# A two-layer graph network with experts on one core: empty rows written between row fetches, and four steps of the routing put elsewhere

## The chip, the cores and the metric

The kernel runs on one core of a Trainium2 chip. The metric is the device time of one execution in microseconds (us); given are the median of the runs and their lowest and highest. A profile of one further execution shows what each engine did. TensorE (PE) does the matmuls, PEld is its loading of weights, VectorE (DVE) and ScalarE (ACT) do elementwise work, GpSimd (POOL) does small work and issues the indirect DMAs, SyncE (SP) issues the plain DMAs.

## The reference

There are N = 2708 nodes with D = 256 features, an adjacency matrix, and E = 8 experts. Each of two layers adds an attention and a mixture of experts to x, each on a normalised x:

```python
    x = x + _L0_gnn_ref(_layernorm(x), adj, ...)    # softmax(q k' / 16 where adj > 0) @ v, then elu
    x = x + _L0_ffn_ref(_layernorm(x)[None], ...)   # 2 of 8 experts, hidden 1024, own layernorm
    x = x + _L1_gnn_ref(_layernorm(x), adj, ...)    # softmax(s_i + s_j + b where adj > 0) @ H
    x = x + _L1_ffn_ref(_layernorm(x)[None], ...)   # 2 of 8 experts, hidden 512
```

An expert is `gelu(x @ W1 + b1) @ W2 + b2`. A gate (x @ Wr, or x @ gate_w) ranks the experts for each node; the two best are applied and their results are added with softmax weights (layer 0: over the two; layer 1: over all eight).

## The kernel before

**Tiles and stages.** The nodes lie in NT = 22 tiles of 128 rows (P), the last with 20. The program runs through layer 0's attention (`layer0_attention`, L293), layer 0's experts, layer 1's attention (`layer1_attention`, L587) and layer 1's experts; two objects of the class `Experts`, `experts0` and `experts1`, hold the experts' parts. `own_norm` is true for layer 0's experts and false for layer 1's.

**Layer 1's attention.** Groups of 6, 6, 4, 3 and 3 tiles of queries are accumulated in PSUM at a time. For each tile of keys k, `attend` issues three matmuls for every query tile of the group (L660: mask times three parts of the values). At a group's end `evict` copies the sums out and gives the group's tiles to the routing (`finish`, which leads into `route`).

**Routing in steps.** `route` (L834) is a generator; each `yield` ends a step. An object of the class `Line` (L264) holds the waiting and the running generators, and each `line.step()` advances every running one by one step and starts a new one at set gaps. In the attention a `line.step()` stands behind the matmuls of each k; in the experts' slots two stand in each slot. So routing and matmuls are woven together by the order of the program. The steps of one tile of nodes are: statistics (L200 to L206; the power L206 is on POOL); the rows written, with the token numbers by POOL (L854) and a copy of the first row into the second (L858, DVE); the gate's logits, the two best and their numbers (L878 to L884) and the exp of the weights (L885, ACT); an empty step; the counting of places by two small matmuls (L899 with `sel`, L900 with `seen`), which share one PSUM tile; and then L901 to L914 on DVE, `seen` being updated by L908, and two indirect scatters by POOL (L917) of the rows into the DRAM buffer `disp`. In `disp` each expert has a region of CAP rows, filled from its start. The row tiles have 4 buffers (pool `routing`), so L854 and L858 of a tile wait for the scatters of an earlier one.

**Tables.** An expert's rows are worked off in slots of 128 rows. `place(s0, s1)` (L924) computes from the counts `seen` (one matmul, L930, then DVE) for the slots s0 to s1 which expert (`weight_row`) and which rows of `disp` (`token_row`) they take. It runs twice for each layer. The early call comes from `begin()` (L1028) in the attention, as soon as 16 tiles (layer 0) or 14 tiles (layer 1) have been routed, for the first n = 24 or 20 slots; these hold only full chunks of rows. `begin` also fetches the rows and weights of slots 0 to 2. The late call comes in a slot, when the routing is finished or when slot n is about to be fetched, for the slots from n on. As an expert's last chunk may be partly filled, the late call also writes, behind the last row of each of the eight experts, 128 rows of "nobody" (L937 to L943: for each expert a register load of the end on SP, L938, and a DMA of 129 KB on SP, L943).

**Slots.** There are up to 50 slots (SLOTS). The weights of a slot lie in one of 4 ring buffers, its rows `xg` in one of 6. Slot s does: `up` (L1128: matmuls `mm`, 16 in layer 1; L1121: the bias copied on ACT; L1136: gelu into `hT` on ACT); a routing step; perhaps `place`; in layer 1 `turned(s + 1)`, which transposes the next slot's rows (L1105, `tp`) and copies them out (L1115 on ACT, `xe`); `down` of slot s - 1 (L1144, eight matmuls in layer 1), with `fetch()` inside; `y` (L1150, L1151 on DVE) and a scatter on POOL (L1155 in layer 1); a routing step. `fetch()` fetches for slot s + 3 (AHEAD) the weights (L1057, indirect, POOL) and the rows (L1067 a register load and L1072 the DMA, SP). The fetch of slot n waits until everything that was written to `disp` has landed; the slots from 3 to n - 1 don't, because their rows are known to be complete. Exp and gelu use different tables of ACT, so an exp between two gelus brings an ACT_TABLE_LOAD ahead of the exp and another ahead of the next gelu.

**What sets the order.** Every engine works off its instructions in order. SP's order is that of the program text everywhere (L74), and in layer 1's slots so are those of PE, ACT and DVE (L1088). Everywhere else a planner of the framework orders each engine's instructions by costs and dependencies.

Of the kernel before, what the change touches and what calls it, by code (L numbers as in the profile page):

```python
# [14 lines left out]
AF = mybir.ActivationFunctionType  # L15
# [4 lines left out]
P = 128  # L20
N = 2708
D = 256
DC = D // P
E = 8
# [24 lines left out]
CAP = (NT + 1) * P  # L49
# [4 lines left out]
AHEAD = 3  # L54
# [6 lines left out]
def adj_ffn_kernel(ctx: ExitStack, tc: tile.TileContext, a: dict, out: bass.AP):  # L61
    nc = tc.nc
# [53 lines left out]
    nobody = const.tile([P, DROW], F32, name="nobody")  # L116
# [470 lines left out]
    def layer1_attention(mTs, kept, line):  # L587
        with ExitStack() as scope:
# [102 lines left out]

            ahead = [normed_rows(t) for t in range(2)]
            cols = columns(0, ahead.pop(0))
            g0, total = 0, None
            for g, wide in enumerate(GROUPS):
                if g == 1:


                    n = FULL_AFTER[experts1.early]
                    experts1.open([i * (n // RING) * E // (n + GROUP) for i in range(RING)])  # L700
                ts_ = list(range(g0, g0 + wide))
                accs = [ps_acc.tile([P, VALUES + 1], F32, name="acc") for _ in ts_]

                line.gap = NT // wide
                for k in range(NT + (LAG1 if g == 0 else 0)):
                    if g == 0:
                        if k + 2 < NT:
                            ahead.append(normed_rows(k + 2))
                        if k < NT:
                            now = cols  # L710
                            if k + 1 < NT:
                                cols = columns(k + 1, ahead.pop(0))
                            values(k, now)
                        if k >= LAG1:
                            attend(ts_, k - LAG1, accs)
                    else:
                        attend(ts_, k, accs)
                        line.step()
                    if g > 0:
                        if not experts1.begun and experts1.routed >= experts1.early:  # L720
                            experts1.begin()
                if g == 0:
                    sums = pool.tile([P, DC], F32, name="sums", bufs=1)
                    nc.vector.tensor_reduce(sums, sums_of, AX.X, ALU.add)
                    total = all_sum(pool, sums, wfc, VALUES, "total1")
                    nc.vector.tensor_add(
                        logits, logits, bfc_gate.unsqueeze(1).to_broadcast([P, NT, E])
                    )
                evict(ts_, accs, total)
                g0 += wide  # L730
# [39 lines left out]
    class Experts:  # L770
        def __init__(self, layer, hidden, packed_weights, w_gate, gate_bias, own_norm, xd, disp, early):
            self.hidden, self.packed_weights, self.own_norm = hidden, packed_weights, own_norm
            self.w_gate, self.gate_bias, self.xd, self.disp = w_gate, gate_bias, xd, disp

            self.seen = const.tile([P, E], BF16, name=f"seen{layer}")
            nc.vector.memset(self.seen, 0.0)
            self.routed, self.begun = 0, False
            self.written = []
            self.groups = [f"written{layer}", f"late{layer}", f"apart{layer}", f"after{layer}"]
            self.early = early  # L780


            n = FULL_AFTER[early]

            size = -(-(SURE - n) // RING)
            runs = [(0, 0, n // RING, 1), (n, size - 1, size, -1)]
            self.number = const.tile([P, SLOTS, 2], F32, name=f"number{layer}")
            number_i = const.tile([P, SLOTS], I32, name=f"number_i{layer}")
            for s0, c0, size, step in runs:
                nc.gpsimd.iota(  # L790
                    number_i[:, s0 : s0 + size * RING], pattern=[[step, size], [size, RING]],
                    base=c0, channel_multiplier=0,
                )
            s0 = n + size * RING
            nc.gpsimd.iota(
                number_i[:, s0:], pattern=[[1, SLOTS - s0]], base=s0 - n, channel_multiplier=0
            )
            nc.vector.tensor_copy(self.number[:, :, 0], number_i)
            nc.vector.tensor_scalar(
                self.number[:, :, 1], self.number[:, :, 0], float(P), None, ALU.mult  # L800
            )
# [32 lines left out]
        def route(self, t, x, logits=None):  # L834


            own_norm, xd, disp, seen = self.own_norm, self.xd, self.disp, self.seen
            w_gate, gate_bias = self.w_gate, self.gate_bias
            r = ROWS[t]
            rows2 = [routing.tile([P, DROW], F32, name=f"row{j}") for j in range(2)]  # L840
# [12 lines left out]
            for j in range(2):  # L853
# [1 line left out]
                    rows2[j].bitcast(I32)[:r, D : D + 1],  # L855
                    token[:r, 0 if own_norm else j, t : t + 1],
                )
            nc.vector.tensor_copy(rows2[1][:r, :D], rows2[0][:r, :D])  # L858
            yield
            lg = small.tile([P, E], F32, name="lg")  # L860
            if logits is None:
# [19 lines left out]
            k = 2 if own_norm else E  # L881
            p = small.tile([P, E], F32, name="p")
            den = small.tile([P, 2], F32, name="den")
            nc.vector.tensor_scalar(p[:r], best[:r], best[:r, 0:1], None, ALU.subtract)  # L884
            nc.scalar.activation(p[:r, :k], p[:r, :k], AF.Exp, accum_out=den[:r, 0:1])  # L885

            hot = small.tile([P, 2, E], F32, name="hot")
            nc.vector.tensor_tensor(
# [5 lines left out]
                nc.vector.memset(sel, 0.0)  # L894
            nc.vector.tensor_add(sel[:r], hot[:r, 0], hot[:r, 1])
            yield
            yield
            ps = misc.tile([P, GROUP, P], F32, name="misc").rearrange("p g n -> p (g n)")
            nc.tensor.matmul(ps[:, :E], before, sel, start=True, stop=False)  # L899
# [21 lines left out]
                )  # L921
            self.routed += 1

        def place(self, s0, s1):  # L924


# [6 lines left out]
            if all_chunks:  # L933

                end = one.tile([P, E], I32, name="end")
                nc.vector.tensor_add(end, n_e, regions)
                for e in range(E):  # L937
                    at = nc.values_load(  # L938
                        end[0:1, e : e + 1], min_val=e * CAP, max_val=e * CAP + N,
                        engines=(mybir.EngineType.SP,),  # L940
                        skip_runtime_bounds_check_because="an expert has at most N tokens",
                    )
                    self.other_rows(nc.sync.dma_start(disp[bass.ds(at, P), :], nobody))  # L943
            tab = one.tile([P, NT, E], F32, name="tab")
            nc.vector.tensor_tensor(
                tab, n_e.unsqueeze(1).to_broadcast([P, NT, E]),
# [20 lines left out]
            n = s1 - s0  # L967
# [129 lines left out]
        def slots(self, two, ps_mm, ps_tp, ps_acc, line):  # L1097
# [20 lines left out]
            def up(w, xe):  # L1118

                bias2 = two.tile([P, D], F32, name="bias2")  # L1120
                (nc.vector.tensor_copy if own_norm else nc.scalar.copy)(bias2, w[:, b2:b1])  # L1121
                hT = two.tile([P, hc, P], F32, name="hT")
                for g in range(0, hc, GROUP):
                    ps = ps_mm.tile([P, GROUP, P], F32, name="mm")
                    for i in range(GROUP):
                        f = g + i
                        for c in range(DC):
                            nc.tensor.matmul(  # L1128
                                ps[:, i, :],
                                w[:, c * hidden + f * P : c * hidden + (f + 1) * P],  # L1130
                                xe[:, c, :],
                                start=(c == 0), stop=(c == DC - 1),
                            )
                    for i in range(GROUP):
                        f = g + i
                        nc.scalar.activation(  # L1136
                            hT[:, f, :], ps[:, i, :], AF.Gelu, bias=w[:, b1 + f : b1 + f + 1]
                        )
                return hT, bias2
# [34 lines left out]
            def slot(s, s1):  # L1174
                nonlocal placed, behind, xe
                w, xg = self.fetched[s]
                if own_norm:
                    xe = turned(s)
                hT, bias2 = up(w, xe)
                line.step()  # L1180

                def fetch():
                    if s + AHEAD < SLOTS and s + AHEAD == len(self.fetched):
                        self.fetched.append((self.fetch_weights(s + AHEAD), self.fetch_rows(s + AHEAD)))

                if not placed and (not line.busy() or s + AHEAD == n):

                    line.finish()
                    self.place(n, SLOTS)
                    placed = True  # L1190

                if s + 1 < s1 and not own_norm:
                    xe = turned(s + 1)
                if behind is None:
                    fetch()
                else:
                    down(*behind, fetch)
                line.step()
                behind = (s, w, xg, hT, bias2)
                if s % 5 == 4 and background:  # L1200
                    background.pop(0)()
# [114 lines left out]
```

## Time and profile before

| | |
|---|---|
| time, median of 3 runs | 1356.41 us (1351.57 to 1359.59) |
| profiled execution, its own time | 1355.36 us |
| span of that execution | 1353.7 us |
| TensorE's mean granted clock | 0.965 |
| busy: PE, DVE, POOL, ACT | 1245.3, 552.6, 415.3, 379.8 us |

The stages lie in that span roughly so: layer 0's attention to 590 us, layer 0's experts to 872, layer 1's attention to 1111, layer 1's experts with routing beside them to 1158, the late tables and the slots around them to 1183, the other slots to 1298, and the end, with the sum of the two parts of each node and the output, to 1353.7.

How to read it: busy times say how much an engine did, not that it was waited for. In the table by windows each row is a stretch of the span, with the time that each engine was busy in it, its granted clock, and the share in which the DMA engines moved data. In the views of groups and of the timeline the square bracket or the last column gives the idle time of the engine just before, and what ended it. The chain of waits goes back from the last instruction through what released each step.

### The profile page before, as it was taken

Reading aid. Unit: us, or ns where it says so; the run is one execution under the profiler, and the core shown is the slowest. Engines: PE = TensorE matmul, PEld = TensorE weight load, DVE = VectorE, ACT = ScalarE, POOL = GpSimd, SP = SyncE. Lnnn points to the kernel's source line nnn. Section 1 sums busy time; section 2 is a strip of 40 time slices with the busy share of each in tenths; the row PEclk is TensorE's granted clock in tenths of the full one; section 3 lists DMA queues with packets and bytes.
Section 4 is the critical chain, followed back from the end, with each engine's and each line's share of the span. In section 5 each row is a group of like instructions: output and inputs, shape, how many; then the busy total and the mean of one; then the engine's idle time right before and its main releaser. Section 6 shows DMA issues by size and latency. Waiting matters only on the chain. (4 is left out here: it accounts for less than half of the span.)

```text
span 1353.7 us, 21527 instructions
## 1 busy us (share of the span) xinstructions
PE 1245.3 (92%) x7536; PEld 973.9 (72%) x7536; DVE 552.6 (41%) x2145; ACT 379.8 (28%) x1134; POOL 415.3 (31%) x523
## 2 busy tenths in 40 slices
PE   7999999999999999999999999879999887599990
PEld 4676666666566666899999999756887647599880
DVE  5723743635527344521221222176546527322124
ACT  3222222212212222633233233234200016344440
POOL 5200110111111212533333333342143437355550
PEclk8899999999999998999999999979999999899995
DMA  6700354997938427275669454360010115434557
GB/s 214 252 5 27 131 178 120 260 230 211 229 89 200 100 68 312 54 240 151 207 210 342 115 165 110 97 223 1 1 40 25 36 52 180 147 102 125 171 173 253
DMA packets 106059, 197.86 MB, mean 146 GB/s; under 512 B 26017, under 2 KB 80374, under 8 KB 99802
## 3 DMA queue, kind: packets, MB, share of 16 engines
q1 hardware_dynamic: 75740, 109.41, 28.4%
q0 software_dynamic: 27392, 84.24, 19.7%
q10 hardware_dynamic: 2814, 2.77, 0.6%
q8 instruction: 62, 1.02, 0.3%
q14 instruction: 51, 0.42, 0.1%
HBM read 263.63 MB, written 66.12 MB: 244 GB/s over the span
## 5 line engine op out<-in xcount | busy, mean ns | idle before, releaser
L1128 PE MATMUL mm<-xe,ring 128*128 128x128 f32 x2192 | 273.8, 279 | 16.9 <-ACT xe L1115 11.6
L1128 PEld LDWEIGHTS mm<-xe,ring 128*128 128x128 f32 x2192 | 264.5, 194 | 33.4 <-ACT xe L1115 14.8
L1144 PE MATMUL acc<-ring,hT 128*128 128x256 f32 x1096 | 267.6, 382 | 3.5 <-ACT hT L1136 3.5
L1136 ACT ACTIVATE hT<-mm,ring 128x128 f32<-128x128 f32 x548 | 156.6, 369 | 256.0 <-issue 185.8
L1144 PEld LDWEIGHTS acc<-ring,hT 128*128 128x128 f32 x1096 | 195.8, 191 | 23.9 <-ACT hT L1136 4.2
L432 PE MATMUL s<-g,xnT 128*128 128x512 f32 x420 | 206.8, 607 | 6.2 <-DVE mT L444 6.2
L489 PE MATMUL acc<-v,p 128*128 128x257 f32 (+1 forms) x880 | 209.0, 389 | 0.0
L1150 DVE TENSOR_TENSOR y<-acc,bias 128x256 f32<-128x256 f32 x92 | 39.0, 424 | 370.3 <-PE acc L1144 357.8
L660 PE MATMUL acc<-parts,mT 128*128 128x265 bf16 (+1 forms) x1386 | 174.5, 282 | 2.1 <-POOL parts L635 1.3
L660 PEld LDWEIGHTS <-mT 128*128 128x128 fp8e4 (+1 forms) x1386 | 132.6, 99 | 49.9 <-issue 22.4
L489 PEld LDWEIGHTS acc<-v,p 128*128 128x128 f32 (+1 forms) x880 | 153.1, 190 | 18.1 <-issue 0.8
L1057 POOL DMA_INDIRECT ring<-L_ffn_packed,weight_row x98 | 104.1, 1062 | 191.7 <-issue 153.2
L206 POOL TENSOR_TENSOR ln_rs<-ln_rs,minus_half 128x2 f32<-128x2 f32 x88 | 67.8, 776 | 237.6 <-DVE ln_rs L202 201.0
L917 POOL DMA_INDIRECT disp<-row,to x88 | 88.1, 1001 | 145.8 <-issue 58.4
L444 DVE TENSOR_SCALAR mT<-s 128x512 fp8e4<-128x512 f32 x105 | 72.0, 687 | 135.1 <-ACT p L443 135.0
L432 PEld LDWEIGHTS s<-g,xnT 128*128 128x128 f32 x420 | 75.8, 193 | 52.8 <-issue 42.1
L443 ACT ACTIVATE p<-s 128x512 f32<-128x512 f32 x105 | 62.2, 595 | 166.6 <-PE s L438 166.4
L1162 POOL DMA_INDIRECT xd<-y,xg x45 | 71.0, 1577 | 87.1 <-PE mm L1128 27.7
L438 PEld LDWEIGHTS <-apart 128*128 128x128 fp8e4 x420 | 32.5, 98 | 60.9 <-issue 60.9
L327 DVE TENSOR_SCALAR apart<-adj 128x677 fp8e4<-128x677 int32 x80 | 40.6, 512 | 50.5 <-DMA adj<-in_adj_dram 43.6
L1155 POOL DMA_INDIRECT xd<-y,xg x47 | 47.2, 1005 | 18.4 <-PE tp L1105 7.0
L854 POOL COPY row<-token 128x1 int32<-128x1 int32 (+1 forms) x88 | 17.4, 209 | 104.2 <-DMA disp<-row,to 103.3
(230 smaller groups left out, 1135.5 us busy)
## 6 DMA issues: line engine op xcount, KB each, us to landing
adj<-in_adj_dram SPq DMA_DIRECT2D x84, 338.5 KB
L_ffn_packed<-in_L_ffn_W_dram SPq DMA_DIRECT2D x16, 1024.0 KB
xg<-disp SPq DMA_DIRECT2D x98, 129.0 KB
L_ffn_packed<-in_L_ffn_W_dram SPq DMA_DIRECT2D x16, 512.0 KB
neighbours<-mT SPq DMA_DIRECT2D x5, 1408.0 KB
mT<-neighbours SPq DMA_DIRECT2D x5, 1408.0 KB
xin<-in_x_dram SPq DMA_DIRECT2D x42, 128.0 KB
ring<-L_ffn_packed SPq DMA_DIRECT2D x4, 1154.0 KB
```

The source lines that it names most:

```text
L206: nc.gpsimd.tensor_tensor(rs[:r, 1], rs[:r, 0], minus_half[:r], ALU.pow)
L432: nc.tensor.matmul(ps[:kr, :nb], xnT[:, c, k0 : k0 + kr], g[:, c, :nb], start=(c == 0), stop=False,)
L443: nc.scalar.activation(p[:kr, :nb], ps[:kr, :nb], AF.Exp, scale=1.0 / 16.0)
L444: nc.vector.tensor_scalar(mT[:kr, k, :], ps[:kr, :nb], -BIG / 2, None, ALU.is_gt, saturate=False,)
L489: nc.tensor.matmul(accs[j][:r], p[keys, q0 : q0 + r], v[keys, k, :], start=(k == 0), stop=(k == NT - 1),)
L660: nc.tensor.matmul(acc[:r], mT[:, k, j * P : j * P + r], parts[:, k, i], start=(k == 0 and i == 0), stop=False,)
L917: nc.gpsimd.indirect_dma_start(disp[:], bass.IndirectOffsetOnAxis(ap=to[:r, j : j + 1], axis=0), rows2[j][:r], None,)
L1057: nc.gpsimd.indirect_dma_start(w, None, packed[:], bass.IndirectOffsetOnAxis(ap=self.weight_row[:, s : s + 1], axis=0), bounds_check=E * P ...
L1128: nc.tensor.matmul(ps[:, i, :], w[:, c * hidden + f * P : c * hidden + (f + 1) * P], xe[:, c, :], start=(c == 0), stop=(c == DC - 1),)
L1136: nc.scalar.activation(hT[:, f, :], ps[:, i, :], AF.Gelu, bias=w[:, b1 + f : b1 + f + 1])
L1144: nc.tensor.matmul(ps, hT[:, f, :], w[:, w2 + f * D : w2 + (f + 1) * D], start=(f == 0), stop=(f == hc - 1),)
L1162: start = nc.gpsimd.indirect_dma_start(xd[:], at, y, None, bounds_check=N - 1, oob_is_err=False, compute_op=ALU.add)
```

## The change

The change has five parts.

1. The writes of "nobody" are not issued in the late `place` any more. A list `pads` keeps them, and `fetch()` issues two of them ahead of its own fetch in each slot, or all that are left where slot s + 3 is n or later. This holds for both layers. In layer 1 they fall two each into slots 9 to 12.
2. The exp of the routing (L885) moves from the step with the two best into the step behind it, which was empty.
3. In layer 1's slots `turned(s + 1)` moves from behind the routing step and the late `place` to ahead of them, so directly behind `up`.
4. In layer 1's attention `begin()` is called two steps of k later. The matmul of the early tables (L930) thus stands behind 14 more of the matmuls L660.
5. The copy of the first row into the second (L858) is done by ACT in layer 1 until `begin()` has run (tiles 0 to 13), and by DVE otherwise, as before.

In the changed kernel the lines have other numbers: the row copy is L859, the exp L899, the nobody rows L928 and L933, the row fetch L1072 and L1077.

```diff
--- before.py
+++ after.py
@@ -691,7 +691,7 @@
 
             ahead = [normed_rows(t) for t in range(2)]
             cols = columns(0, ahead.pop(0))
-            g0, total = 0, None
+            g0, total, since = 0, None, 0
             for g, wide in enumerate(GROUPS):
                 if g == 1:
 
@@ -716,8 +716,9 @@
                     else:
                         attend(ts_, k, accs)
                         line.step()
-                    if g > 0:
-                        if not experts1.begun and experts1.routed >= experts1.early:
+                    if g > 0 and not experts1.begun and experts1.routed >= experts1.early:
+                        since += 1
+                        if since > 2:
                             experts1.begin()
                 if g == 0:
                     sums = pool.tile([P, DC], F32, name="sums", bufs=1)
@@ -774,7 +775,7 @@
 
             self.seen = const.tile([P, E], BF16, name=f"seen{layer}")
             nc.vector.memset(self.seen, 0.0)
-            self.routed, self.begun = 0, False
+            self.routed, self.begun, self.pads = 0, False, []
             self.written = []
             self.groups = [f"written{layer}", f"late{layer}", f"apart{layer}", f"after{layer}"]
             self.early = early
@@ -855,7 +856,9 @@
                     rows2[j].bitcast(I32)[:r, D : D + 1],
                     token[:r, 0 if own_norm else j, t : t + 1],
                 )
-            nc.vector.tensor_copy(rows2[1][:r, :D], rows2[0][:r, :D])
+            (nc.vector.tensor_copy if own_norm or self.begun else nc.scalar.copy)(
+                rows2[1][:r, :D], rows2[0][:r, :D]
+            )
             yield
             lg = small.tile([P, E], F32, name="lg")
             if logits is None:
@@ -882,7 +885,6 @@
             p = small.tile([P, E], F32, name="p")
             den = small.tile([P, 2], F32, name="den")
             nc.vector.tensor_scalar(p[:r], best[:r], best[:r, 0:1], None, ALU.subtract)
-            nc.scalar.activation(p[:r, :k], p[:r, :k], AF.Exp, accum_out=den[:r, 0:1])
 
             hot = small.tile([P, 2, E], F32, name="hot")
             nc.vector.tensor_tensor(
@@ -894,6 +896,7 @@
                 nc.vector.memset(sel, 0.0)
             nc.vector.tensor_add(sel[:r], hot[:r, 0], hot[:r, 1])
             yield
+            nc.scalar.activation(p[:r, :k], p[:r, :k], AF.Exp, accum_out=den[:r, 0:1])
             yield
             ps = misc.tile([P, GROUP, P], F32, name="misc").rearrange("p g n -> p (g n)")
             nc.tensor.matmul(ps[:, :E], before, sel, start=True, stop=False)
@@ -921,6 +924,14 @@
                 )
             self.routed += 1
 
+        def pad(self, end, e):
+            at = nc.values_load(
+                end[0:1, e : e + 1], min_val=e * CAP, max_val=e * CAP + N,
+                engines=(mybir.EngineType.SP,),
+                skip_runtime_bounds_check_because="an expert has at most N tokens",
+            )
+            self.other_rows(nc.sync.dma_start(self.disp[bass.ds(at, P), :], nobody))
+
         def place(self, s0, s1):
 
 
@@ -934,13 +945,7 @@
 
                 end = one.tile([P, E], I32, name="end")
                 nc.vector.tensor_add(end, n_e, regions)
-                for e in range(E):
-                    at = nc.values_load(
-                        end[0:1, e : e + 1], min_val=e * CAP, max_val=e * CAP + N,
-                        engines=(mybir.EngineType.SP,),
-                        skip_runtime_bounds_check_because="an expert has at most N tokens",
-                    )
-                    self.other_rows(nc.sync.dma_start(disp[bass.ds(at, P), :], nobody))
+                self.pads = [partial(self.pad, end, e) for e in range(E)]
             tab = one.tile([P, NT, E], F32, name="tab")
             nc.vector.tensor_tensor(
                 tab, n_e.unsqueeze(1).to_broadcast([P, NT, E]),
@@ -1177,9 +1182,16 @@
                 if own_norm:
                     xe = turned(s)
                 hT, bias2 = up(w, xe)
+
+                if s + 1 < s1 and not own_norm:
+                    xe = turned(s + 1)
                 line.step()
 
                 def fetch():
+
+                    for _ in range(2 if s + AHEAD < n else E):
+                        if self.pads:
+                            self.pads.pop(0)()
                     if s + AHEAD < SLOTS and s + AHEAD == len(self.fetched):
                         self.fetched.append((self.fetch_weights(s + AHEAD), self.fetch_rows(s + AHEAD)))
 
@@ -1188,9 +1200,6 @@
                     line.finish()
                     self.place(n, SLOTS)
                     placed = True
-
-                if s + 1 < s1 and not own_norm:
-                    xe = turned(s + 1)
                 if behind is None:
                     fetch()
                 else:
```

## The prediction

> **What bounds the kernel now.** I read the page first, then the table by windows, and then, for each window in which TensorE is not full, what it waited for.
>
> ```profile
> PE 1245.3 (92%) x7536; PEld 973.9 (72%) x7536; DVE 552.6 (41%) x2145; ACT 379.8 (28%) x1134; POOL 415.3 (31%) x523
> ```
>
> TensorE is the bound: 92% of the span. A change can only win the other 8%, and the matmuls that ran at a lower clock. The windows (span, PE busy, ..., then the granted clock) say where these lie:
>
> ```profile
> 590.00:872.00 282.00, 281.70 (x1923) 258.72 (x1923) 60.63 (x192) 88.08 (x308) 102.88 (x81) 1.00 0.59 181
> 1010.00:1111.00 101.00, 91.11 (x726) 66.03 (x723) 49.54 (x308) 6.47 (x33) 41.07 (x63) 0.95 0.13 41
> 1111.00:1162.00 51.00, 38.80 (x269) 34.64 (x270) 32.48 (x157) 33.28 (x82) 32.99 (x39) 1.00 0.40 134
> 1162.00:1183.00 21.00, 10.01 (x57) 8.60 (x56) 4.37 (x18) 3.53 (x12) 4.72 (x5) 0.76 0.63 199
> 1183.00:1250.00 67.00, 67.00 (x466) 62.71 (x465) 14.00 (x36) 32.60 (x108) 37.05 (x36) 1.00 0.34 103
> ```
>
> 590 to 872 is layer 0's experts: full. 1010 to 1111 is the end of layer 1's attention, 1111 to 1162 its slots 0 to 9, which still carry routing, 1162 to 1183 slots 10 and 11 around the late tables, and from 1183 the slots run full at 3.73 us each (up 1.78, turn 0.22, down 1.73). The three windows between are what the change can touch.
>
> In attention, the groups by line name the waits; the PE timeline gives each and what followed it:
>
> ```profile
> L900 PE MATMUL misc<-seen,ones 128*128 128x8 bf16 x16 | 2.7, 166 | 6.5 <-DVE seen L908 6.5
> L930 PE MATMUL misc<-seen,ones 128*128 128x8 bf16 x1 | 0.2, 166 | 2.8 <-DVE seen L908 2.8
> ```
>
> ```profile
> 1073.41 0.17 PE L900 MATMUL misc<-seen,ones 128*128 128x8 bf16 x1 [3.57 <-DVE seen L908]
> 1073.44 4.80 PE L660 MATMUL acc<-parts,mT 128*128 128x265 bf16 x27
> ...
> 1086.01 0.17 PE L930 MATMUL misc<-seen,ones 128*128 128x8 bf16 x1 [2.78 <-DVE seen L908]
> ```
>
> A warm run of 63 of these matmuls takes 7.41 us, so 27 take 3.18; they took 4.80. Each of the three waits (2.95, 3.57, 2.78) is followed by about 1.63 us lost to the clock.
>
> At the late tables I read the chain of waits:
>
> ```profile
> 1160.23 0.17 DVE end L936
> ...
> 1167.48 0.33 SPq L943
> 1167.86 0.41 SPq L1067
> ...
> 1168.45 0.44 SPq L1072
> 1168.91 9.69 DMA xg<-disp
> ...
> 1178.74 0.66 PE tp L1105 x2
> ```
>
> SP writes eight tiles of "nobody" (L938 register load and L943, about 0.85 us a pair), only then fetches the rows of slot 12; they land 9.69 us later, and TensorE stood 9.35 us before turning them. The eight down matmuls behind took 3.51 us where 1.89 is usual: 1.62 more.
>
> In slots 1 to 9 ScalarE is the late one, since each exp costs two table loads:
>
> ```profile
> 1133.69 1.28 ACT L1136 ACT_TABLE_LOAD   x1 [3.08 <-PE tp L1105]
> ...
> 1138.62 1.28 ACT L1136 ACT_TABLE_LOAD   x1 [0.32 <-PE mm L1128]
> ```
>
> The first had counting matmuls (L899/L900) between up and turn and began 3.08 us late; the second, with the turn directly behind up, 0.32.
>
> **What the Trainium skill says.** "TensorE: Matmul & The Clock Gate", Part 1: a PE idle for a free-running window of about 3.4 us falls to half clock, and needs as long to come back. The trace agrees roughly: waits of 2.78 to 3.57 and of 9.35 cost 1.62 or 1.63 us each, one of 2.35 cost nothing. "ScalarE: Activation LUTs", What ACT_TABLE_LOAD costs: 1283 ns, and 1380 of drain; the trace has the 1283, and no such drain (the activation starts within 0.1 us). "DMA: Bandwidth & Descriptors", Anatomy of one DMA: 2.0 us plus bytes over 436 GB/s. For 129 KB an estimate of 2.3 us; the trace's 9.69 is that transfer in traffic, and decides for traffic.
>
> **The change, part by part.**
>
> *Rows of nobody, two per slot (layer 1).* Removed from before slot 12's fetch: six pairs, 6 x 0.85 = 5.1 us of SP. In the changed kernel's instruction order SP has two pads and a fetch, four times (slots 9 to 12, rows 12 to 15); the fetches of slots 12 to 19 wait for no pad to land. Before, rows(12) were issued 11.0 us after slot 9's start (1168.91 - 1157.90). Now: tables at +2.3, two pads, loads: +5.7. Needed: after slots 9, 10, 11's up, about +11.6 (slot 10 stays long, 5.54 us, because the tables' 5.1 us of DVE work delay y and so the bias, an ACT wait of 4.11). Cover 5.9 us. Landing: bounds 2.3 (the skill's price, empty queues) and 9.7 (before). In the 9.7, eight pads (1.03 MB) and two weight gathers (2 x 1.15 MB) were in flight: 3.4 MB at 350 GB/s is 9.8 us, so the traffic explains it. Now two pads, a remainder of one gather and the rows are ahead, about 0.6 MB: 1.7 + 2.0 = 3.7 us, an estimate. I take "under 5.9": the 9.35 and the 1.62 go, **-11.0**. The other six pads cost SP 1.7 us per slot of 3.73, and then 0.9 for the fetch: hidden by the slot; without that cover up to 1.7 each. What is late next is ScalarE in slot 10, already counted.
>
> *The same in layer 0.* PE is busy 281.70 of 282 there, so SP's eight pads are hidden before, and two per slot of 7.3 us after: **0**; bounds 0 and +1.
>
> *Exp a step later, turn ahead of the routing's step.* By the instruction order, all exps in slots now stand behind the copy xe of the next slot, and the turn directly behind up; one exp more than before (six, not five) falls into slots. Before, the slots with order xe, exp, bias took 4.93 us (3.73 + 1.2), those with hT, exp, xe and the counting matmuls cost some 4.0 (slots 3 and 4: 1.49 + 2.36; 6 and 7: 1.49 + 2.70). Slots 0 to 9 took 1112.32 to 1161.80 = 49.5. Now 3.55 for slot 0, six of 4.93 and three of 3.73: 44.3. **-5**; bounds 0 (the new exp placed as badly) and -6. What now waits behind the turn of the next slot on PE are the counting matmuls and, in slot 9, L930; the turn's rows were fetched three slots ahead, and slots 1 to 9 show no wait of a turn for rows, so that costs 0.22. On ACT in attention the later exp has cover, for ACT is 6% busy there (6.47 of 101); without it L901 and the scatters would come a step later.
>
> *Row copies on ScalarE.* 14 copies (tiles 0 to 13) of 288 ns leave DVE, in attention. An ACT copy takes about 0.37 (L1115), hidden by its idle time: 0. Removed from the chain L206, L858, L908 that feeds the waits: 0.2 to 0.3 a step; the wait of the copy for the scatter's landing goes over to L903. So it is worth little by itself.
>
> *Tables two steps later.* L930 moves behind 14 more L660 matmuls: 14 x 0.139 = 1.95 us of cover for its wait. POOL's gathers and SP's row fetches of slots 0 to 2 move too, past two more scatter pairs on POOL (2 x 2 x 1.0 us); rows were issued at 1092.76 and needed at 1111.32, so 18 us of cover against some 2 to 6: 0.
>
> *The attention waits together.* Replayed by hand with the new DVE order: the first stays (2.95, +0.3); the second falls from 3.57 to about 1.9, below what cooled the PE, -1.6 - 1.6; PE comes 3 us earlier to the third, for which "seen" is 1.4 earlier and 1.95 of cover new: 2.78 to about 2.3. Sum -3.3 to -4.9: I take **-4**. Bounds: 0 (the chain moves with PE, since it hangs on POOL and on landings) and -10 (both waits and their clock gone: 3.57 + 2.78 + 2 x 1.63).
>
> Sum: -11 - 5 - 4 = **-20**. The profiled execution took 1355.36 (span 1353.7): 1335.4. It lies 1.05 below the median, so against 1356.41: **1336.4**.
>
> **Rivals.**
> (a) The rows still land 9.7 us after issue, since landing depends on the weights' traffic and not on pads. 3.8 + 1.6 remain: 1342 (1341 to 1344). For it: 199 GB/s and 0.63 DMA share in that window. Against: far fewer bytes ahead.
> (b) Only the placement pays; the attention waits move with the chain, and the sixth exp's two table loads (2.6) eat the slots' gain: 1356.4 - 11 = 1345 (1344 to 1352).
> (c) All attention waits stay under what cools the PE: -10 instead of -4: 1330 (1326 to 1331).
> (d) Slower: the pads now stand ahead of four row fetches. If each of these lands later than its cover, the stall comes four times: with 9.7, (3.8 + 1.6) x 4 = 21.6 against 20 gained, +1.6; with 12, 31 against 20: 1367. It decides from about 9.3 us of landing in all four slots. Against: each carries only 0.26 MB of pads.
> That the change does nothing is excluded by the instruction order.
>
> **Chances.** The likeliest (1331 to 1341): 0.50. (a) 0.17, (b) 0.13, (c) 0.15, (d) 0.05. A measurement here tells 0.5% (6.8 us) from no change: faster is below 1349.6, which is all but 0.03 of (b) and (d): 0.92; same 0.03 + 0.02 of (d); slower 0.03. The range, 1329 to 1346, leaves out the lower part of (c), half of (b), and (d): 0.17.
>
> **What would show it.** SP's L933 in pairs between L1077 (the row fetch after the change); no PE idle of microseconds before the turn of slot 12, and slot 12 starting about 20 us earlier than 1182.54; exp slots of 4.93 and no late ACT table load on the turn; L900 and L930 waiting together under 7 us instead of 9.3; 590 to 872 as before. A wait before the turns of slots 13 to 15 would make me wrong, as would attention waits that keep their size, or slots with exps above 5.2 us.

## The result and the profile after

The changed kernel took 1346.63 us (median of 7 runs, 1341.71 to 1347.52), the kernel before beside it 1355.48 (7 runs): ratio 0.9926, 95% interval 0.9906 to 0.9946. On the median that the prediction started from, 1356.41, that is 1346.4, or -10.0, where -20 was forecast. The profiled execution after took 1346.34 (span 1344.6), 9.1 less in span than the one before.

The same windows of the changed kernel (span, PE busy, ..., granted clock, DMA share, GB/s):

```profile
590.00:872.00 282.00, 280.80 (x1918) 257.77 (x1916) 61.72 (x194) 86.92 (x304) 104.24 (x81) 1.00 0.59 179
1010.00:1111.00 101.00, 91.56 (x726) 68.10 (x725) 49.39 (x303) 15.11 (x52) 38.59 (x60) 0.94 0.12 39
1111.00:1162.00 51.00, 39.78 (x236) 35.29 (x235) 31.75 (x153) 29.76 (x72) 32.25 (x38) 0.89 0.41 133
1162.00:1183.00 21.00, 17.36 (x119) 15.71 (x120) 6.84 (x25) 8.32 (x28) 10.25 (x11) 1.00 0.73 229
```

The window of the late tables is mended: 17.36 busy of 21 where it was 10.01. But 1111 to 1162, where the slots with routing lie, now has a clock of 0.89 where it had 1.00, and only 236 matmul records where it had 269. Windows at fixed times mix stages once everything has moved, so I took the starts of the ups from the PE timelines:

| stage | before | after | change |
|---|---|---|---|
| start to the end of layer 1's first group | 970.5 | 966.8 | -3.7 |
| layer 1's groups 1 to 4, to slot 0 | 141.8 | 137.4 | -4.5 |
| slots 0 to 9 | 49.5 | 58.6 | **+9.1** |
| slots 10 and 11 | 20.7 | 8.8 | **-11.9** |
| slots 12 to 19 | 30.1 | 32.3 | +2.3 |
| the rest | 141.1 | 140.7 | -0.4 |

The first row is no effect of the change that I could show: in the profiles of the other runs (listed under Experiments) the same point lies between 965.6 and 975.9.

**The late tables.** SP's timeline after, and the PE timeline at the turn and the up that follow:

```profile
1161.03 1.28 SPq L933 DMA_DIRECT2D disp<-nobody  x2
1165.24 0.01 SPq L1077 DMA_DIRECT2D xg<-disp  x1
1166.03 1.16 SPq L933 DMA_DIRECT2D disp<-nobody  x2
1168.21 0.35 SPq L1077 DMA_DIRECT2D xg<-disp  x1
```

```profile
1169.60 0.38 PE L1110 MATMUL tp<-ident,xg 128*128 128x128 f32 x2
...
1177.56 2.02 PE L1133 MATMUL mm<-xe,ring 128*128 128x128 f32 x16 [1.70 <-DMA ring<-L_ffn_packed,weight_row]
```

Rows 12 are issued 7.4 us after slot 9's start (1157.85), not 11.0, and the turn at 1169.60 has no idle in front: they landed within 4.4. What is late next is not rows but weights: slot 13 waits 1.70 for them. The chain of waits shows that gather under way for 8.69 us, nearly as long as the rows before (9.69):

```profile
1168.50 8.69 DMA ring<-L_ffn_packed,weight_row
```

**Attention.** The waits on `seen` after, with the matmuls behind two of them:

```profile
1037.86 0.17 PE L903 MATMUL misc<-seen,ones 128*128 128x8 bf16 x1 [2.94 <-DVE seen L911]
1037.89 7.07 PE L660 MATMUL acc<-parts,mT 128*128 128x265 bf16 x60
...
1057.52 0.17 PE L903 MATMUL misc<-seen,ones 128*128 128x8 bf16 x1 [0.32 <-DVE seen L911]
...
1068.69 0.17 PE L903 MATMUL misc<-seen,ones 128*128 128x8 bf16 x1 [3.72 <-DVE seen L911]
1068.71 5.93 PE L660 MATMUL acc<-parts,mT 128*128 128x265 bf16 x27
```

Three waits of 6.98 together where there were 9.30. The last of them, 3.72, stands at the same matmul as the second before, 3.57 (the one with 27 matmuls behind it), so that wait did not fall; the 0.32 is new, one step earlier. L941 (the early tables' matmul, the third wait before) waits no more. "Warm" means at full clock here: a wait of 2.94 cost no clock this time (60 matmuls in 7.07, the warm time), one of 3.72 cost 2.75 (27 in 5.93 where 3.18 is warm).

**Slots 0 to 9.** DVE, then ACT, then PE of the changed kernel:

```profile
1110.26 0.16 DVE L904 RECIPROCAL den<-den 128x1 f32<-128x1 f32 x1 [7.13 <-ACT p L899]
...
1116.79 0.41 DVE L212 TENSOR_SCALAR row<-kept,ln_mv,ln_rs 128x256 f32<-128x256 f32 x1 [3.72 <-POOL ln_rs L206]
```

```profile
1117.94 0.41 ACT L1126 COPY bias<-ring 128x256 f32<-128x256 f32 x1 [4.29 <-issue]
...
1130.25 1.28 ACT L1141 ACT_TABLE_LOAD   x1 [2.91 <-PE acc L1149]
...
1149.58 1.28 ACT L1141 ACT_TABLE_LOAD   x1 [3.01 <-PE acc L1149]
```

```profile
1133.01 3.79 PE L1133 MATMUL mm<-xe,ring 128*128 128x128 f32 x16 [3.39 <-ACT xe L1120]
...
1152.33 3.38 PE L1133 MATMUL mm<-xe,ring 128*128 128x128 f32 x16 [3.48 <-ACT xe L1120]
```

Three things are to be seen. The sixth exp falls into slot 0, behind the first gelu; VectorE, in written order, stands 7.13 us for it, and with it the whole routing of the next tiles, so that POOL's power comes later too (3.72), y behind that, and the bias on ACT (4.29). The two slots that were long, 4 and 7, are still long (7.53 and 7.62, before 6.09 and 6.43): their gelu's table load begins at 1130.25 and 1149.58, where up ended at 1127.53 and 1146.76; that is behind the end of down (1129.61 and 1148.84). And behind the idles that follow, 3.39 and 3.48, TensorE is slow: ups of 3.79 and 3.38 where a warm one behind a wait took 2.05. Before, the longest idle here was 2.35, and no up was slow.

That is not the whole of the slow matmuls. The ups of slots 0 and 1 are slow too, behind idles of 0.51 and 1.04:

```profile
1104.14 3.03 PE L1133 MATMUL mm<-xe,ring 128*128 128x128 f32 x16 [0.51 <-ACT xe L1120]
...
1108.66 3.55 PE L1133 MATMUL mm<-xe,ring 128*128 128x128 f32 x16 [1.04 <-ACT xe L1120]
```

The windows from the start of slot 0 to the start of slot 10, before and after, split the loss (span, then PE busy; the third figure from the end is the granted clock):

```profile
1112.32:1161.80 49.48, 38.19 (x265) 34.25 (x266) 32.09 (x155) 32.86 (x81) 32.79 (x39) 1.00 0.41 137
1104.14:1162.72 58.58, 45.61 (x266) 40.97 (x266) 33.11 (x161) 35.71 (x85) 32.66 (x39) 0.85 0.36 118
```

For the same matmuls TensorE was busy 7.4 us longer, at a lower clock; its idle time grew by only 1.7, from 11.3 to 13.0. So what the later exp and the earlier turn do to the waits themselves is the smaller part of the 9.1 in this profile; how much of the slow clock is theirs is a question for the experiments.

### The profile page after: what moved, and what is told of

Read it like the earlier page. It is cut to its first block, busy times and chain, and to the rows that moved or that the text cites. A ratio compares the mean times of both kernels' runs of the same rounds, so it can differ in the third digit from the quotient of the medians.

```text
span 1344.6 us, 21529 instructions
## 1 busy us (share of the span) xinstructions
PE 1244.8 (93%) x7536; PEld 977.8 (73%) x7536; DVE 551.1 (41%) x2131; ACT 388.3 (29%) x1150; POOL 413.7 (31%) x523
## 5 line engine op out<-in xcount | busy, mean ns | idle before, releaser
L1133 PE MATMUL mm<-xe,ring 128*128 128x128 f32 x2192 | 280.1, 283 | 17.9 <-ACT xe L1120 10.6
L1133 PEld LDWEIGHTS mm<-xe,ring 128*128 128x128 f32 x2192 | 270.5, 197 | 33.2 <-ACT xe L1120 13.0
L660 PE MATMUL acc<-parts,mT 128*128 128x265 bf16 (+1 forms) x1386 | 171.8, 280 | 2.1 <-POOL parts L635 1.3
L660 PEld LDWEIGHTS <-mT 128*128 128x128 fp8e4 (+1 forms) x1386 | 131.7, 98 | 45.7 <-issue 19.1
```

The lines of the kernel that those rows point to most:

```text
L660: nc.tensor.matmul(acc[:r], mT[:, k, j * P : j * P + r], parts[:, k, i], start=(k == 0 and i == 0), stop=False,)
L1133: nc.tensor.matmul(ps[:, i, :], w[:, c * hidden + f * P : c * hidden + (f + 1) * P], xe[:, c, :], start=(c == 0), stop=(c == DC - 1),)
```

## Experiments

Theory A: the loss of 9 us in slots 0 to 9 comes from the later exp and the earlier turn, by the order that they make. Theory B: it is where stretches of half clock ("clock windows") happened to fall in that execution. Ratios are to the kernel before in the same batch; the last column is the time of slots 0 to 9 in the run's one profile.

| run | parts of the change | ratio (95%) | slots 0 to 9 |
|---|---|---|---|
| (before) | none | 1 | 49.5 |
| (after) | all | 0.9926 (0.9906 to 0.9946) | 58.6 |
| again | all | 0.9929 (0.9906 to 0.9951) | 56.9 |
| u_turn | all but the turn | 0.9951 (0.9934 to 0.9968) | 56.7 |
| u_exp | all but the exp | 0.9930 (0.9907 to 0.9953) | 53.8 |
| u_turn_exp | rows of nobody, copies, tables | 0.9898 (0.9873 to 0.9924) | 51.2 |
| best | the same | 0.9904 (0.9883 to 0.9924) | 48.7 |
| p_pads | rows of nobody | 0.9940 (0.9918 to 0.9961) | 49.2 |
| p_tables | rows of nobody, tables | 0.9932 (0.9909 to 0.9955) | 53.8 |
| p_copies | rows of nobody, copies | 0.9919 (0.9895 to 0.9943) | 52.3 |
| u_pads | all but the rows of nobody | 1.0006 (0.9985 to 1.0026) | 55.4 |
| s_behind | all, step behind down | 0.9900 (0.9880 to 0.9921) | 56.5 |
| s_behind_exp | all but the exp, step behind down | 0.9903 (0.9880 to 0.9926) | 53.4 |
| pow3 | all, power three times | 0.9978 (0.9964 to 0.9992) | 59.9 |

**Undoing the turn, the exp, both; and the rows of nobody alone.** The edits put lines back where they were:

```diff
-                if s + 1 < s1 and not own_norm:      # u_turn: below the late place again
-                    xe = turned(s + 1)
                 line.step()
```
```diff
+            nc.scalar.activation(p[:r, :k], ...)     # u_exp: behind L887 again
-            nc.scalar.activation(p[:r, :k], ...)     # and gone from L899
```

u_turn:

> The changed kernel with the turn of the next rows put back behind the routing's step (the other four parts stay). Theory A (the loss of 9.1 us in slots 0 to 9 has two sources: counting matmuls that now stand directly ahead of down, so that the next gelu is released only after down; and the sixth exp, which falls into slot 0): the first source goes. Slots 4 and 7 fall from 7.53 and 7.62 to about 6.3, and the stretches at half clock behind them (2.8 and 1.3 us) go, so about 6 us faster than the changed kernel: 1340.5. Rival B (the loss is the free-running clock window that happened to fall badly): within 2 us of the changed kernel, either sign.

u_exp:

> The changed kernel with the exp put back into the step with the two best (the other four parts stay). Theory A: five exps in the slots, not six; DVE does not wait 7.13 us for the first exp in slot 0, and slots 0 to 2 give back about 3 us; the slots with counting directly ahead of down stay long. About 1343.5. Rival B: within 2 us of the changed kernel. Rival C (the later exp is what shortened the attention's waits): slower than the changed kernel, as the attention gives back up to 4.5.

u_turn_exp:

> The changed kernel with both the turn and the exp put back: only the nobody rows, the row copy on ScalarE and the later early tables stay. Theory A: slots 0 to 9 as before the change, 49.5 instead of 58.6, all else as in the changed kernel: about 9 us faster than it, 1337.5. Rival B: within 2 us of it. Rival C: slots as before, but the attention's 4.5 lost too: about 1342.

p_pads:

> The kernel before with only the nobody rows put two per slot ahead of the fetches. Theory A and the prediction: the wait of 9.35 before the turn of slot 12 and the 1.62 behind it go, -11 to -12 us: 1344. Rival B: the same, plus or minus the clock's 2 us. A result near 1355 would say that the placement's gain in the changed kernel comes from elsewhere.

Neither undone alone is faster than the whole change (0.9951 and 0.9930 against 0.9926). A missed there: u_turn was to be 6 us faster than the whole change and is some 3 slower by the ratios, u_exp was to be 3 faster and is level; both differences lie inside the intervals. Both undone are faster: 0.9898, 3.8 us below the whole change, where A said 9. The four runs here stand beside each other on one chip, so two more comparisons can be made. Against u_turn_exp, the later exp alone (u_turn) costs 7 us, 0.9951 against 0.9898, with intervals that are apart; the earlier turn alone (u_exp) costs 4, 0.9930, with intervals that overlap. With both (the whole change) the loss is not the sum of the two. C (of u_exp's expectation) falls: with the exp put back the attention's groups took 135.4, not more than 137.4. The rows of nobody alone give -8.1 (0.9940 of 1351.71; 5.3 to 11.1 by the interval), where -11 to -12 was expected.

**The step behind down; the other two parts alone.**

```diff
                 if s + 1 < s1 and not own_norm:
                     xe = turned(s + 1)
-                line.step()
+                if own_norm:
+                    line.step()
...
                     down(*behind, fetch)
                 line.step()
+                if not own_norm:
+                    line.step()
```

p_tables leaves the copy on VectorE and p_copies calls `begin()` at once; both also have exp and turn where they were.

s_behind:

> The changed kernel, and in layer 1's slots the first routing step also moved behind down, so that both steps of a slot stand there and no counting matmul stands between an up and its down. Theory A (release of gelu held where counting matmuls stand in the stream ahead of down): no slot above 5.5 us but the first three and slot 9; slots 0 to 9 fall from 58.6 to about 51 to 53 (the two long slots, 7.5 and 7.6, give 2.5 each, and the clock stretches behind them 2 to 3), so some 6 us below the changed kernel, 15 to 16 below the kernel before. Rival B (clock windows fall at random): slots 0 to 9 stay near 58, 9 below the kernel before.

s_behind_exp:

> As the step behind down, with the exp put back into the step with the two best. Theory A, with the later exp as the larger part of the loss (slots 0 to 9 were 4.8 us shorter with the exp put back): slots 0 to 9 about 47, 20 below the kernel before. If the later exp was a loss only by the slots it fell into, not by its place, this equals the step behind down alone.

p_tables:

> The kernel before with the nobody rows two per slot and the early tables two steps later, nothing else. As forecast, the later tables give 1.95 us of cover to the third wait: it falls from 2.78 to about 0.8, and the clock stretch behind it (1.63) goes: 3 us below the nobody rows alone, 11 to 13 below the kernel before. If the chain moves with PE, equal to the nobody rows alone (8 to 11 below).

p_copies:

> The kernel before with the nobody rows two per slot and the row copies of tiles 0 to 13 on ScalarE, nothing else. Forecast: little by itself, within 1 us of the nobody rows alone; the second wait on seen stays above 3 us. If the copies carry the attention's gain (with copies and later tables the second wait fell from 3.57 to 0.2), the second wait is under 1 us here too and the time 3 to 5 us below the nobody rows alone.

s_behind is nearly as fast as A said (0.9900; 13.6 below the kernel before, where A said 15 to 16), but by another road: its slots 0 to 9 took 56.5, close to B's 58. Slots 4 and 7 are shorter (5.56 and 5.97, where 7.53 and 7.62 were), slot 6 is longer (6.09, where 4.86 was), and slot 9, the only one left with a small matmul between turn and down, L941, took 11.38. Its ACT and PE timelines:

```profile
1156.49 1.28 ACT L1141 ACT_TABLE_LOAD   x1 [7.05 <-remote]
```

```profile
1150.26 0.17 PE L941 MATMUL misc<-seen,ones 128*128 128x8 bf16 x1
1150.28 1.97 PE L1149 MATMUL acc<-ring,hT 128*128 128x256 f32 x8
1159.24 3.79 PE L1133 MATMUL mm<-xe,ring 128*128 128x128 f32 x16 [6.99 <-ACT xe L1120]
```

So a late table load came again in a slot with a small matmul between turn and down, and no longer in slots 4 and 7, where it now stands behind down. (In the profile of the changed kernel slot 9 has L941 in the same place and is short, 4.87: such a matmul isn't enough.) With the exp put back as well, slots 0 to 9 are 3 us shorter in the profile (A said 47, it is 53.4), the time the same (0.9903, where A said 20 us below the kernel before).

Tables alone and copies alone can't be told from the rows of nobody alone (-1.1 and -2.8 us of 1355, inside the intervals, and from another batch). The two together are 5 to 6 us faster by the ratios, 0.9898 and 0.9904 against 0.9940, with intervals that just overlap. How long each wait on `seen` is can't be had from single profiles: u_turn_exp and best are the same program, and their second and third waits were 0.20 and 2.71, and 2.93 and 1.09; p_copies had 0.47 and 4.40, p_tables 3.65 and none. What one gains the other loses. Their sum is steadier: 6.35, 5.46 and 4.87 in the three profiles without the later tables ((before), p_pads, p_copies), and 2.6 to 4.3 in the eleven with them. So the profiles say that the later tables shorten this pair of waits; no pair of runs shows it in the time.

**The whole change once more, the fastest so far once more, and the change without its first part.** u_pads issues the eight writes in the late `place` again.

again:

> The changed kernel once more, for a second profile of it and as the measure for the others beside it. Theory A (the long slots have causes in the program's order): slots 0 to 9 again 56 to 59, with slots 4 and 7 above 7 and the gelu's table load released only after down. Rival B (they come and go with the execution): slots 0 to 9 differ from 58.6 by over 3, and the long slots are others.

best:

> Nobody rows, row copies on ScalarE and later tables, exp and turn where they were: the fastest so far, once more on the same chip as the changed kernel. Theory A: 4 to 7 us below the changed kernel, with slots 0 to 9 at 49 to 52. Rival B: equal to it within 2.

u_pads:

> The changed kernel with the eight writes of nobody issued together in the late tables as before; the other four parts stay. If the placement is what the change gains (about -10 of 9), this is 9 to 11 us slower than the changed kernel, about level with the kernel before (0 to 2 above it), with an idle of 8 to 10 before the turn of slot 12.

Slots 0 to 9 took 56.9 in the second profile, with slot 4 at 6.75 and slot 7 at 8.46, and VectorE stood 7.64 for the exp: B, as it was put (other long slots, and a sum that differs by over 3), falls. But a part of B stands. Here are the same windows of again and of best:

```profile
1110.43:1167.30 56.87, 44.33 (x266) 39.32 (x266) 32.98 (x161) 35.82 (x85) 32.59 (x39) 0.88 0.37 121
1114.05:1162.80 48.75, 38.19 (x266) 34.27 (x267) 32.16 (x155) 32.91 (x81) 33.00 (x39) 1.00 0.42 139
```

In again TensorE is busy 6.1 longer than before, and at other places: its slow ups are those of slots 0, 3 and 8, in the first profile those of 0, 1, 5 and 8. In best no up is slow, but in u_turn_exp, the same program, two are, and TensorE is busy 3.1 longer than before. A slow up of slot 0 stands in eleven of the thirteen profiles of changed kernels, p_tables and p_copies among them, which have exp and turn where they were. So slow stretches of this kind come without the exp and the turn too; how much of the slow clock is due to those two, no run separates.

best is 0.9904, 3.4 us below the change beside it; with the first pair (u_turn_exp, 3.8, against the first measurement of the change) that makes two pairs, each with intervals that overlap. Its slots 4 and 7 begin the table load 0.70 and 1.09 behind the end of up, earlier than before the change (1.29 and 1.63), and not 2.7 and 2.8 behind as after it:

```profile
1134.62 1.28 ACT L1141 ACT_TABLE_LOAD   x1 [2.50 <-PE tp L1110]
...
1151.22 1.28 ACT L1141 ACT_TABLE_LOAD   x1 [2.80 <-PE tp L1110]
```

u_pads is level with the kernel before, and 10.5 above the changed kernel by the ratios. SP's eight writes and the wait are back, in a kernel that has everything else:

```profile
1164.71 8.97 SPq L933 DMA_DIRECT2D disp<-nobody  x8
1174.31 17.18 SPq L1078 DMA_DIRECT2D xg<-disp  x5
```

```profile
1182.31 0.66 PE L1111 MATMUL tp<-ident,xg 128*128 128x128 f32 x2 [8.99 <-DMA xg<-disp]
1182.77 3.62 PE L1150 MATMUL acc<-ring,hT 128*128 128x256 f32 x8
```

**What the late release hangs on.** TensorE tells the other engines that a group of matmuls is done by an update of a semaphore; this is the release that the next gelu waits for. In the trace's semaphore events the updates of up, turn, counting and down of slot 4 after come in one burst, at 1130.18 to 1130.36, while up had ended at 1127.53 and the next matmuls are recorded as running on (their ends are modelled in this view). At most of the bursts, in this and the other profiles, POOL's power was just ending, or its last scatter had ended some 1.5 us before.

```diff
-        nc.gpsimd.tensor_tensor(rs[:r, 1], rs[:r, 0], minus_half[:r], ALU.pow)
+        for _ in range(times):                       # 3 in routing behind the early tables
+            nc.gpsimd.tensor_tensor(rs[:r, 1], rs[:r, 0], minus_half[:r], ALU.pow)
```

pow3:

> The changed kernel, where each power (L206) of the routing behind the early tables is computed three times by POOL instead of once (the same value): 1.5 us more on POOL for each tile. In twelve long slots seen, TensorE's releases came in one burst within 1 us of POOL's power or of its last scatter. If they hang on what POOL is doing, the bursts come about 1.5 us later in the slots with counting ahead of down (4 us behind up instead of 2.7). If not, they stay at 1.2 to 2.7 behind up, and the time grows only by what the powers hold up on VectorE (up to 1.5 for each of 8 tiles).

Neither way. The kernel is about 6.7 slower than the change (0.9978 against 0.9929), and VectorE waits longer for the power (4.50, 2.99, 3.25, 4.16 in its timeline), but slots 4 and 7, which have the order that was long, lost the late release: the table load begins 0.54 behind the end of up in slot 4, and right behind the bias in slot 7.

```profile
1139.71 1.28 ACT L1142 ACT_TABLE_LOAD   x1 [0.73 <-PE misc L904]
...
1157.51 0.41 ACT L1127 COPY bias<-ring 128x256 f32<-128x256 f32 x1 [1.24 <-issue]
1157.93 1.28 ACT L1142 ACT_TABLE_LOAD   x1
```

So the order alone doesn't make it late. What else it takes, and what holds the release, stays open.

## Why the prediction was right, and where it was wrong

The sum, -10 where -20 was forecast, lies at the upper edge of the range (1346.4 against 1329 to 1346) and outside the likeliest part of it (1331 to 1341). It lies there mainly because one term of the sum had the wrong sign.

- **Rows of nobody, -11.0: right in the wait, a little high in the time.** Measured -8.1 alone (5.3 to 11.1), 10.5 within the change, and 11.9 in the profile of slots 10 and 11. Rows of slot 12 were issued 7.4 us after slot 9's start, not 5.7, which left 4.4 us and not 5.9; they landed within that, so the estimate of 3.7 was low by at most 0.7. The price of 2.3 that the prediction takes from the Trainium skill ("DMA: Bandwidth & Descriptors", Anatomy of one DMA) is given there for transfers that GpSimd issues; these are SyncE's. Rivals (a) and (d) fell: no turn waited for rows. Not seen: the weights of slot 13 (1.70, and slots 12 to 19 longer by 2.3); "what is late next is ScalarE in slot 10, already counted" failed there.
- **Layer 0, 0: right.** 280.80 of 282 busy.
- **Attention, -4: near in sum** (-4.5 in the profile, -3.1 in again's; but -1.9 of it also in p_pads, whose attention is that of before). The second and third waits were forecast at 1.9 and 2.3, together 4.2; together they were 3.7 and 3.2 in the two profiles, but each time one was as long as ever (3.72 and none, 0.47 and 2.73). Which one that is, the replay could not say; that the sum came out is in part luck.
- **Exp and turn, -5: wrong.** This is the step that failed: "six of 4.93 and three of 3.73". Measured: slots +9.1 and +7.4 in two profiles of the change, and about +3.6 in time (0.9926 and 0.9929 against 0.9898 and 0.9904). Not all of the slots' loss reaches the time in these pairs; single profiles also differ elsewhere by 2 to 3. By the prediction's own sign (slots with exps above 5.2 us) it was wrong here: slots 3, 4 and 7 took 5.8, 7.5 and 7.6. The price of 4.93 was taken from slots in which the exp came from a tile whose data was ready and in which no counting stood ahead of down; slot 2, with the same order but an exp that waited for its data, had taken 5.42 before. Three assumptions under it failed. First, that the sixth exp costs only its two table loads (2.6): it stands in slot 0 behind the first gelu, and VectorE's written order waits for it (7.13 and 7.64) with all that follows. Second, that counting matmuls delay gelu only between up and turn: between turn and down the release came 2.65 and 2.74 behind up, where 1.22 and 1.56 were. (That the new place lengthens it isn't shown: with the turn in its old place p_copies has a load 2.6 behind up in slot 7.) Third, that the slots run at full clock: it took nothing for slow matmuls there, and they are 7.4 of the 9.1 in the first profile, 6.1 of the 7.4 in the second. In time, the later exp alone is shown to cost (7 us against both undone); of the turn, and of how the two combine to 3.6, the runs do not say more.
- **Rival (b)** described the outcome best: 1345, "the sixth exp's two table loads eat the slots' gain". It had the right place and too small a price, and it took the attention for nothing, where the profiles gave 3 to 4.5.

The fastest versions are the change without its parts 2 and 3, and the change with the routing's step behind down (0.9898 to 0.9904): 13 us below the kernel before.

## What to carry to other kernels

Where several engines run in a written order, an operation that is moved one step later moves the wait of everybody who is queued behind its reader: list these before pricing the operation itself. A long transfer wait can be a queue problem: look at what was issued just ahead, and spread what nobody needs yet; then look at which transfer is the next in the same traffic. A price that was measured in one arrangement of instructions holds for that arrangement only, and matmuls that run at a lower clock can cost more than the waits that one counts.

## What the runs showed of the hardware

An idle of TensorE does not have one price. The Trainium skill ("TensorE: Matmul & The Clock Gate", Part 1) says that the window that decides on half clock runs freely, and these traces agree: waits of 2.95 and 2.94 at the same matmul cost 1.63 in one execution and nothing in another, one of 3.72 cost 2.75. In u_exp an idle of 3.37 behind slot 4 was followed by an up of 2.05, which is warm. Nor does it take a long idle: the up of slot 0 took 2.93 to 3.68 in eleven profiles, behind idles of 0.51 or 0.59, and 2.05 in the other three behind the same idles. So idles below 2.35, which cost nothing in the profile that the prediction read, can be followed by slow matmuls.

The releases that TensorE gives can come late, in one burst, though its matmuls are recorded as running on: by 2.65 us behind up in slot 4, and by 6.5 in slot 9 of s_behind. In the fourteen profiles the bursts of three or four updates over 1 us behind an up of layer 1 lie in slots 4, 7 and 9 alone, slots in which a small bf16 matmul stands between the fp32 ones of up and down; not every such slot has a burst, and the trace names no cause.
